# Attention and a clustering block on one core: stacking the first keys and queries inside SBUF, and moving five small steps of the attention

## The chip, the core and the metric

The kernel runs on one core of a Trainium2 chip, in one launch. The metric is the device time in microseconds (us); lower is better. The profile is one more execution, taken by the hardware profiler, with every instruction's start and end on each engine: PE is TensorE (matmuls; PEld its weight loads), DVE is VectorE, ACT is ScalarE, POOL is GpSimd, and SP is SyncE, which here only issues transfers. ACT and POOL can issue transfers too. "SPq", "ACTq" are the instructions with which an engine issues a transfer.

## The reference

Four images x of 256 channels and 64 x 64 points go through two layers. The first is self-attention over all 4096 points of an image, the second a clustering block with two group norms, an MLP and a pointwise convolution. All is float32.

```python
# layer 0, per image, xf = x as 256 x 4096
q = jnp.einsum('oc,bcn->bno', wq, xf) + bq              # 32 numbers a point
k = jnp.einsum('oc,bcn->bon', wk, xf) + bk[None, :, None]
attn = softmax(jnp.einsum('bnd,bdm->bnm', q, k), axis=-1)   # 4096 x 4096
v = jnp.einsum('oc,bcn->bon', wv, xf) + bv[None, :, None]
out = jnp.einsum('bcn,bmn->bcm', v, attn)
x = gamma[0] * out + x
# layer 1
y = x + ls1 * cluster(group_norm(x), ...)
y = y + ls2 * mlp(group_norm(y))
z = relu(batch_norm(y * dw_w)); z = relu(batch_norm(conv1x1(z, pw_w)))
```

The change touches only layer 0 (queries, keys, scores, softmax, and the product with the values).

## The kernel before, in words

The whole order of the work is written out by hand: each engine executes its instructions in the order of the program, and an engine waits (with everything behind it) until its next instruction may start. The compiler framework adds the waits, from which instruction writes or reads which tile.

**Queries and keys (L326 to L355).** For one image, the 4096 points are 8 blocks of 512 (`NB`). A projection (`projected`, L331) puts four blocks under each other, 32 rows each, into one 128 x 512 PSUM tile, so two projections of keys (i = 0, 1) and two of queries cover an image. `halves_of` splits each into a high part (float32r, ACT, L348) and a rest (DVE, L349), and writes four copies in a fixed pattern of high and low to DRAM (L355, four transfers of 256 KB). `k_unit` (L411) and `q_block` (L405) read one block back, whose 32 rows then lie interleaved by four on 128 partitions. One float32r matmul over these 128 rows gives the score with the cross terms of the two parts.

**Scores.** A unit u is one query block nb = u // 8 with one key block g = u % 8; there are 64 units an image (`units`). `half(u, h)` makes half of a unit's scores: two matmuls into one of the two `ps_s` PSUM buffers (`products`, L433), a copy to SBUF by ACT (`kept`, L446), and a running maximum over the keys by DVE (`highest_of`, L457), kept in the tile `top`. Starting unit u (`begun`) also issues the load of keys u + 1; the two `k` buffers alternate, so that load waits until PE is through with unit u - 1. A half that is "kept only" takes its maximum later, from the SBUF copy; such operations stand in the list `held`, and `caught(n)` issues the next n of them on DVE. `fold` (L514) catches all that are left and ends the maximum of a query block.

**The start (`alone`), image 0 only.** The value pairs (`v_pair`, L388: eight matmuls and an ACT copy L396; 16 pairs in all) 0 to 2, then `staged` (projection 0 of keys and queries, with its DRAM copies), the first loads of k and q, pairs 3 to 7, the sums of values that the product needs (`sums(g)`, four POOL operations L608 for each of 8 groups), then eight units of scores. In the first of them stand the second projections (`halved`, tag `t13`), and between them pairs 8 to 15, and the other weights (`load_rest`, a generator that issues a few SP transfers with every `next`; its last step has two POOL operations on the pointwise weights). Images 1 to 3 do this work inside the layer 1 of the image before.

**The weighting.** `weighting` runs 64 units. PE multiplies the values with the exponentials by a scheme of seven products for eight (`weigh`, parts 0 to 3, L678), from which results `av` are evicted by ACT at the end of a query block (`evict`, L708) and combined by POOL (`combined`, L719 to L724). In unit u, `exps(u + 1)` subtracts the maxima (DVE, L599 twice; the maxima lie in half of the PSUM tile `hold`, which takes one of the two `ps_s` buffers) and takes exponentials (ACT, L603 to L605), and `factors(u + 1)` forms the sums: t on DVE (L622), s and t4 on POOL (L608), and the running sum of the denominators `acc` (POOL). Between the parts the scores of later units are put in (`due`): two halves a unit, three in units 1, 3, 7 and 9, which are then kept only.

**Maxima and denominators of a block.** For query blocks from the third on, `highest(nb + 1)` (in unit g = 5 and 6) reduces `top` across partitions through small transposes in the tile `few`, writes 512 numbers to DRAM (L99) and reads them back on all partitions (`mr`, L100); ACT copies `mr` into `hold` (L582). `total(nb - 1)` does the same with the denominators, from g = `when` on. `few` takes the buffer of the weights `mix` (pool `swap`); the first call of `spare`, which is in `total(0)` in unit 10, lets POOL clear it (L539). `leave` multiplies by the denominators (POOL, L748), `sent` stores the result to DRAM (SP, L756).

**The tail.** In the last dozen units `load` (L106, SP) brings x in again, `shift` (ACT, L766) adds a constant, and `back` (POOL's queue, accumulating) adds the stored result.

Of the kernel before, what the change touches and what calls it, by code (L numbers as in the profile page):

```python
# [8 lines left out]
F32 = mybir.dt.float32  # L9
F32R = mybir.dt.float32r  # L10
# [4 lines left out]
P = 128  # L15
# [3 lines left out]
NB = 512  # L19
# [41 lines left out]
def attention_then_cluster_block(  # L61
# [101 lines left out]
    def load_rest():  # L163
        load_mix("first")
        yield
        nc.sync.dma_start(out=fvb[:, ED:], in_=v_b.partition_broadcast(P))
        nc.sync.dma_start(out=wproj_s[:ED], in_=wproj)
        nc.sync.dma_start(out=wproj_s[ED:, :], in_=pc[:, ipb : ipb + 1].rearrange("c o -> o c"))
        yield
        for i, f in enumerate(behind):  # L170
            f()
            if i == 2:
                yield
        nc.gpsimd.tensor_tensor(pw_q[1], pw_q[1], pw_q[3], ALU.add)
        nc.gpsimd.tensor_scalar(pw_q[3], pw_q[3], -1.0, None, ALU.mult)
        yield
# [88 lines left out]
    def wf():  # L265

        tps = ps_m.tile([P, NB], F32, tag="m", name="wf_p")
        for k in range(KC):
            nc.tensor.transpose(
                tps[:ED, k * P : (k + 1) * P], own_w["mix"][:, k, 0, 16 : 16 + ED], ident  # L270
            )
        nc.tensor.matmul(tps[:, C : C + ED], fb_w, ident[:ED, :ED], start=True, stop=True)
        nc.scalar.copy(wf_t, tps[:ED, :C])
        nc.scalar.copy(fvb[:, :ED], tps[:, C : C + ED])
# [43 lines left out]
    def attention(b, xs, ys):  # L318
# [7 lines left out]
        def projected(which, i, ps):  # L326

            col = 1 if which == "k" else 0
            for k in range(KC):
                for r in range(RG):  # L330
                    nc.tensor.matmul(  # L331
                        ps[r * D : (r + 1) * D],
                        wqk_s[:, k, col],
                        block(xs, k, 4 * i + r),
                        start=(k == 0),
                        stop=(k == KC - 1),
                    )

        def halves_of(which, i, hi, lo, ps, dma=nc.sync):

            col = 1 if which == "k" else 0
            if which not in own:
                own[which] = dram.tile([NBLK // RG, P, 4, NB], F32, tag=which, name=f"{which}_{b}")
            bias = bqk_s[:, col : col + 1]
            nc.scalar.activation(hi, ps, AF.Identity, bias=bias)  # L348
            nc.vector.scalar_tensor_tensor(  # L349
                lo, ps, bias, hi.bitcast(F32), ALU.add, ALU.subtract  # L350
            )
            rows = own[which][i]
            for c in range(4):
                part = hi if c in ((0, 2) if which == "k" else (0, 1)) else lo
                dma.dma_start(out=rows[:, c], in_=part.bitcast(F32))  # L355

        def stacked(which, nb):

            i, r = divmod(nb, RG)
            return own[which][i, r * D : (r + 1) * D].rearrange("d c n -> (d c) n")  # L360

        def staged(name, which, dma=nc.sync):


            st = spool.tile([P, 4, NB], F32R, tag="s", name=f"st_{b}_{name}")
            ps = ps_s.tile([P, 2, NB], F32, tag="s", name=f"pr_{b}_{name}")
            for j, (w, i) in enumerate(which):
                projected(w, i, ps[:, j])
            for j, (w, i) in enumerate(which):
                halves_of(w, i, st[:, 2 * j], st[:, 2 * j + 1], ps[:, j], dma)  # L370

        def halved(which, i):

            ps = ps_m.tile([P, NB], F32, tag="m", name=f"{which}p_{b}_{i}")
            two = work.tile([P, 2, NB], F32R, tag="t13", name=f"hl_{which}_{b}_{i}")
            projected(which, i, ps)
            halves_of(which, i, two[:, 0], two[:, 1], ps)

        vps = {}

# [17 lines left out]
        def v_pair(i):  # L398
            v_half(2 * i)
            v_half(2 * i + 1)  # L400

        def q_block(nb):

            qs[nb] = work.tile([P, NB], F32R, tag="q", name=f"q_{b}_{nb}")
            nc.sync.dma_start(out=qs[nb].bitcast(F32), in_=stacked("q", nb))  # L405

        def k_unit(u):

            g = u % GRP
            ks[u] = big.tile([P, NB], F32R, tag="k", bufs=2, name=f"k_{b}_{u}")  # L410
            nc.sync.dma_start(out=ks[u].bitcast(F32), in_=stacked("k", g))  # L411

        def begun(u):

            if u in slots:
                return
            nb, g = divmod(u, GRP)
            if u + 1 < units:
                k_unit(u + 1)

            pool, tag = {SLOTS: (swap, "w1"), SLOTS + 1: (swap, "w2")}.get(
                u % (SLOTS + 2), (spool, "s")
            )
            slots[u] = pool.tile([P, 4, 2, QW], F32, tag=tag, name=f"s_{b}_{u}")
            if g == 0:
                tops[nb] = work.tile([P, 2, NB], F32, tag="top", bufs=1, name=f"top_{b}_{nb}")
# [18 lines left out]
        def kept(u, h, sc):  # L445
            nc.scalar.copy(slots[u][:, PAIR[h]].rearrange("p h r n -> p r h n"), tiles(sc))  # L446
# [314 lines left out]
        def load(i):  # L761
            ys.append(load_x(b, i))
# [46 lines left out]
        def alone():  # L809

            roots()
            for i in range(3):
                v_pair(i)
            staged("first", (("k", 0), ("q", 0)))
            k_unit(0)
            q_block(0)
            q_block(1)
            for i in range(3, 8):
                v_pair(i)
            for g in range(4):  # L820
                for f in sums(g):
                    f()
            for u in range(GRP):
                if u == 0:
                    begun(0)
                    halved("k", 1)
                    halved("q", 1)
                    rest = load_rest()
                half(u, 0)()
                if u < GRP - 1:  # L830
                    half(u, 1)()
                else:

                    sc = products(u, 1)
                    highest_of(0, tiles(sc))
                    kept(u, 1, sc)
                    v_pair(14)
                if u < 6:
                    v_pair(u + GRP)
                elif u == 6:  # L840
                    wf()
                if u > 1:
                    next(rest, None)
            fold(0)
            for g in range(4, GRP - 1):
                for f in sums(g):
                    f()
            tp = turned_over(0, ps_m.tile([P, 4, P], F32, tag="m", name=f"tt_{b}_0"))
            half(GRP, 0)
            dgs["dg"] = across(0, "w2", tp)  # L850
            spread(0, dgs["dg"])
            v_pair(15)
            exps(0)
            factors(0)
            half(GRP, 1, True)
            for f in sums(GRP - 1):
                f()
# [32 lines left out]
        def weighting(next_x, fill, early, begin):  # L890
# [6 lines left out]
            def tail(u):  # L897


                for at_u, f in (  # L900
                    (units - 12, lambda: load(0)),
                    (units - 11, lambda: load(1)),
                    (units - 10, lambda: (load(2), back(0))),
                    (units - 9, lambda: (load(3), back(1))),
                    (units - 8, lambda: back(2)),
                    (units - 5, lambda: (next_x(), next_x())),
                    (units - 4, lambda: (load_mix(b), next_x())),
                    (units - 4, lambda: b == B - 1 and load_mlp(b)),
                    (units - 3, lambda: (next_x(), begin())),
                    (units - 2, lambda: b < B - 1 and load_mlp(b)),  # L910
                ):
                    if u == at_u:
                        f()

            for u in range(units):
# [12 lines left out]
                maxima = due(u, 0)  # L928
                if more and nb and g == GRP - 2:
                    next(peak)  # L930
                    sent(nb - 1)
                if g == GRP - 1 and more:
                    gather(nb)
# [4 lines left out]
                if nb < 2 or g == 6:  # L938
                    caught(1)

                when = 1 if nb > 1 else 2
                if nb and g == when:
                    den = total(nb - 1)
                    next(den)
# [4 lines left out]
                    next(peak)  # L949
                if early and nb > 1:  # L950
                    early.pop(0)()
                if u in views:
                    pooled(views[u])
                    seen(views[u], (0,))
# [36 lines left out]
                    f()  # L991
                if nb and g == when:
                    next(den)
                elif nb and g == (4 if more else 3):
                    leave(nb - 1)
                elif nb and g == 4 and not more:
                    sent(nb - 1)
                if (u, 0) in at and (u, 1) in at:
                    caught(1)
                weigh(u, av, 3)  # L1000
                if g == 3 and nb + 2 < NBLK:
                    q_block(nb + 2)
# [1058 lines left out]
```

## Time and profile before

| | us |
|---|---|
| median of three runs | 3167.59 (3166.77 to 3168.53) |
| profiled execution, its own time | 3166.07 |
| its span from first to last instruction | 3164.3 |
| PE busy in the span | 3058.6 |
| DVE, POOL, ACT busy | 2510.8, 2321.1, 1779.7 |
| start to the last maximum of the first query block | 66.5 |
| a unit of weighting, from block 2 on | 7.0 |
| 256 KB of keys from DRAM, issue to landing | 2.7 |

A row of the timeline gives the start, the duration (of a merged piece: from its first start to its last end), the engine, the line in the code, the operation, "written<-read", the shapes, the count, and in brackets how long the engine had stood idle and which engine's instruction ended the wait. In the groups and waits the releaser is the one that came last by the profile. The clock column is the share of the full TensorE clock that was granted.

### The profile page before, as it was taken

Reading aid. Unit: us, or ns where it says so; the run is one execution under the profiler, and the core shown is the slowest. Engines: PE = TensorE matmul, PEld = TensorE weight load, DVE = VectorE, ACT = ScalarE, POOL = GpSimd, SP = SyncE. Lnnn points to the kernel's source line nnn. Section 1 sums busy time; section 2 is a strip of 40 time slices with the busy share of each in tenths; the row PEclk is TensorE's granted clock in tenths of the full one; section 3 lists DMA queues with packets and bytes.
Section 4 is the critical chain, followed back from the end, with each engine's and each line's share of the span. In section 5 each row is a group of like instructions: output and inputs, shape, how many; then the busy total and the mean of one; then the engine's idle time right before and its main releaser. Section 6 shows DMA issues by size and latency. Waiting matters only on the chain.

```text
span 3164.3 us, 41331 instructions
## 1 busy us (share of the span) xinstructions
PE 3058.6 (97%) x14210; PEld 2499.2 (79%) x14210; DVE 2510.8 (79%) x3574; ACT 1779.7 (56%) x2817; POOL 2321.1 (73%) x2216
## 2 busy tenths in 40 slices
PE   7999999999999999999999999999999999998999
PEld 5788888788678888778867888887877788885786
DVE  3889888677788888877778888787778888887675
ACT  4566664544556666454555666644555666655444
POOL 3888888377488888647758888855866888893663
PEclk9999999999999999999999999999999999999999
DMA  5112126100111222610011211441011122150000
GB/s 166 44 58 64 54 64 191 60 28 28 44 44 57 67 61 87 168 57 18 28 50 48 66 56 58 120 129 57 28 40 44 54 61 64 57 150 3 14 21 27
DMA packets 105875, 200.41 MB, mean 63 GB/s; under 512 B 14416, under 2 KB 30400, under 8 KB 104128
## 3 DMA queue, kind: packets, MB, share of 16 engines
q1 hardware_dynamic: 101856, 181.94, 18.1%
q0 software_dynamic: 2976, 14.70, 2.4%
q8 instruction: 113, 1.85, 0.2%
q10 hardware_dynamic: 832, 1.11, 0.1%
q14 instruction: 98, 0.80, 0.1%
HBM read 149.37 MB, written 48.34 MB: 62 GB/s over the span
## 4 chain that ended last, share of the span: by engine, by line
PE 68%; POOL 14%; DVE 10%; issue 3%; DMA 2%; ACT 2%; SPq 0%; POOLq 0%; ACTq 0%; DVEq 0%
PE av L678 29%; PE mo L1673 10%; PE sc L433 6%; POOL acc L608 5%; PE hq L1756 5%; PE hp L1756 3%; POOL t L608 3%; PE hr L1756 3%; PE fv L1245 3%; POOL s L608 2%; DVE top L457 2%; PE vp L388 2%; DVE s L599 1%; PE mo L1657 1%; DVE t L622 1%
## 5 line engine op out<-in xcount | busy, mean ns | idle before, releaser
L446 ACT COPY s<-sc 128x1024 f32<-128x1024 f32 x512 | 515.0, 1011 | 419.5 <-PE sc L433 411.0
L599 DVE TENSOR_TENSOR s<-s,hold 128x1024 f32<-128x1024 f32 x512 | 598.7, 1209 | 12.4 <-ACT hold L582 10.3
L608 POOL TENSOR_TENSOR acc<-acc,t 128x512 f32<-128x512 f32 x408 | 536.2, 1334 | 0.0
L678 PE MATMUL av<-s,v 128*128 128x256 f32 x2048 | 526.1, 379 | 6.6 <-ACT t L708 4.0
L678 PE MATMUL av<-s,sum 128*128 128x256 f32 x2048 | 526.8, 380 | 3.6 <-POOL s L608 3.4
L678 PE MATMUL av<-t,v 128*128 128x256 f32 x2048 | 526.8, 380 | 1.8 <-POOL t L608 1.8
L608 POOL TENSOR_TENSOR s<-t,s 128x512 f32<-128x512 f32 x256 | 339.7, 1327 | 251.5 <-DVE t L622 184.7
L622 DVE TENSOR_TENSOR t<-s,hold 128x1024 f32<-128x1024 f32 x256 | 312.0, 1219 | 205.3 <-POOL acc L608 108.7
L678 PEld LDWEIGHTS av<-s,v 128*128 128x128 f32 x2048 | 386.9, 189 | 70.3 <-ACT t L708 5.6
L433 PE MATMUL sc<-q,k 128*128 128x512 f32 x1024 | 395.1, 470 | 47.6 <-DVE top L457 27.9
L457 DVE TENSOR_TENSOR top<-sc,top 128x1024 f32<-128x1024 f32 x350 | 426.6, 1219 | 14.4 <-ACT s L446 10.4
L678 PEld LDWEIGHTS av<-t,v 128*128 128x128 f32 x2048 | 387.7, 190 | 61.5 <-POOL t L608 6.5
L678 PEld LDWEIGHTS av<-s,sum 128*128 128x128 f32 x2048 | 388.1, 190 | 60.9 <-POOL s L608 8.4
L1711 ACT ACTIVATE hs<-hs,pv_s 128x256 f32<-128x256 f32 x496 | 232.5, 502 | 352.5 <-DVE hs L1747 352.5
L1673 PE MATMUL mo<-hs,w 128*128 128x256 f32 x1512 | 384.8, 381 | 0.0
L608 POOL TENSOR_TENSOR t<-s 128x512 f32<-128x512 f32 x256 | 340.6, 1331 | 47.1 <-PE av L678 34.1
L1673 PEld LDWEIGHTS mo<-hs,w 128*128 128x128 f32 x1512 | 283.7, 190 | 46.9 <-ACT hs L1711 6.3
L603 ACT ACTIVATE hold<-s 128x512 f32<-128x512 f32 x256 | 154.1, 602 | 245.7 <-DVE s L599 245.3
L433 PEld LDWEIGHTS sc<-q,k 128*128 128x128 f32 x1024 | 175.0, 191 | 143.2 <-DVE top L457 85.4
L605 ACT ACTIVATE s<-s 128x1024 f32<-128x1024 f32 x256 | 266.8, 1042 | 0.0
L1747 DVE TENSOR_TENSOR hs<-hq,hs 128x256 f32<-128x256 f32 x496 | 198.7, 421 | 85.7 <-PE hq L1756 75.4
L678 PE MATMUL av<-t,sum 128*128 128x256 f32 x1024 | 262.4, 378 | 0.0
(292 smaller groups left out, 4862.3 us busy)
## 6 DMA issues: line engine op xcount, KB each, us to landing
k<-k SPq DMA_DIRECT2D x256, 256.0 KB, 2.7
x<-in_x SPq DMA_DIRECT2D x62, 512.0 KB, 5.6
out<-xn SPq DMA_DIRECT2D x62, 256.0 KB, 2.1
att<-t SPq DMA_DIRECT2D x56, 256.0 KB, 4.1
x<-att POOLq DMA_DIRECT2D x12, 1024.0 KB, 9.0
q<-q SPq DMA_DIRECT2D x32, 256.0 KB, 4.1
w<-in_w SPq DMA_DIRECT2D x8, 1024.0 KB, 12.0
k<-hl_k SPq DMA_DIRECT2D x28, 256.0 KB, 2.6
```

The costliest lines, as they stand in the source:

```text
L433: nc.tensor.matmul(sc[:, r, :], k_s[:, (2 * h + r) * P : (2 * h + r + 1) * P], qs[u // GRP], start=True, stop=True,)
L446: nc.scalar.copy(slots[u][:, PAIR[h]].rearrange("p h r n -> p r h n"), tiles(sc))
L457: nc.vector.tensor_tensor(top, src, top if saved[nb] is None else saved[nb], ALU.max)
L599: nc.vector.tensor_tensor(sh, sh, mb.to_broadcast([P, 2, 2, QW]), ALU.subtract)
L605: nc.scalar.activation(s[:, PAIR[1]], s[:, PAIR[1]], AF.Exp)
L608: nc.gpsimd.tensor_tensor(out, x, y, op)
L622: nc.vector.tensor_tensor(t31[u], s[:, B11 : B22 + 1 : 2], b12.to_broadcast([P, 2, 2, QW]), ALU.add)
L678: nc.tensor.matmul(av[bank][:, half_ * QW : (half_ + 1) * QW], a[:, r], t[:, r], start=(g == 0 and r == 0 and i in (1, 7, 2, 4)), stop=(g ...
L1673: return nc.tensor.matmul(bank[:, half * HB : (half + 1) * HB], a[:, j], t, start=start, stop=stop)
L1711: nc.scalar.activation(src, src, AF.Gelu_apprx_tanh, bias=pvc("b1", P, j + 4 * (i > 1)))
L1747: nc.vector.tensor_tensor(dst, ps, term, ALU.add)
L1756: nc.tensor.matmul(out, w, x, start=True, stop=True)
```

## The change

Five things are done, in the functions printed above.

- **Start.** `staged` no longer writes the first keys and queries to DRAM and reads them back: four transfers from SBUF to SBUF of 32 rows each (`straight`) put k_0, four q_0 (two of these issued by ACT) and four k_1 in place. The copies in DRAM are written after that (`written`), for the other blocks. The second projections stand in units 0 and 1, value pairs 6 and 7 too; later pairs, group 3's sums, q_1's load and `load_rest` are placed anew.
- **`spare()`** is called in unit 4 of the weighting.
- **First denominators:** `when` is 3, not 2, for query block 1; their `leave` is in g = 5, not 4.
- **Held maxima:** the `caught(1)` at the end of the units with three halves (1, 3, 7, 9) is gone.
- **`load(1)`** is called in unit 54, after the read of `mr` has been issued and ahead of `sent`, not at the end of unit 53.

```diff
--- before.py
+++ after.py
@@ -336,7 +336,7 @@
                         stop=(k == KC - 1),
                     )
-        def halves_of(which, i, hi, lo, ps, dma=nc.sync):
+        def halves_of(which, hi, lo, ps):
@@ -349,32 +349,54 @@
             nc.vector.scalar_tensor_tensor(
                 lo, ps, bias, hi.bitcast(F32), ALU.add, ALU.subtract
             )
+        def part_of(which, c, hi, lo):
+            return (hi if c in ((0, 2) if which == "k" else (0, 1)) else lo).bitcast(F32)
+        def written(which, i, hi, lo):
             rows = own[which][i]
             for c in range(4):
-                part = hi if c in ((0, 2) if which == "k" else (0, 1)) else lo
-                dma.dma_start(out=rows[:, c], in_=part.bitcast(F32))
+                nc.sync.dma_start(out=rows[:, c], in_=part_of(which, c, hi, lo))
         def stacked(which, nb):
             i, r = divmod(nb, RG)
             return own[which][i, r * D : (r + 1) * D].rearrange("d c n -> (d c) n")
-        def staged(name, which, dma=nc.sync):
-            st = spool.tile([P, 4, NB], F32R, tag="s", name=f"st_{b}_{name}")
-            ps = ps_s.tile([P, 2, NB], F32, tag="s", name=f"pr_{b}_{name}")
-            for j, (w, i) in enumerate(which):
-                projected(w, i, ps[:, j])
-            for j, (w, i) in enumerate(which):
-                halves_of(w, i, st[:, 2 * j], st[:, 2 * j + 1], ps[:, j], dma)
+        def staged():
+            st = spool.tile([P, 4, NB], F32R, tag="s", name=f"st_{b}")
+            ps = ps_s.tile([P, 2, NB], F32, tag="s", name=f"pr_{b}")
+            both = {"k": (st[:, 0], st[:, 1]), "q": (st[:, 2], st[:, 3])}
+            for j, w in enumerate("kq"):
+                projected(w, 0, ps[:, j])
+            def straight(w, dst, r, other=nc.sync):
+                for c in range(4):
+                    (other if c % 2 else nc.sync).dma_start(
+                        out=dst[c::4].bitcast(F32), in_=part_of(w, c, *both[w])[r * D : (r + 1) * D]
+                    )
+            for g in range(2):
+                ks[g] = big.tile([P, NB], F32R, tag="k", bufs=2, name=f"k_{b}_{g}")
+            qs[0] = work.tile([P, NB], F32R, tag="q", name=f"q_{b}_0")
+            halves_of("k", *both["k"], ps[:, 0])
+            straight("k", ks[0], 0)
+            halves_of("q", *both["q"], ps[:, 1])
+            straight("q", qs[0], 0, nc.scalar)
+            straight("k", ks[1], 1)
+            for w in "kq":
+                written(w, 0, *both[w])
         def halved(which, i):
             ps = ps_m.tile([P, NB], F32, tag="m", name=f"{which}p_{b}_{i}")
             two = work.tile([P, 2, NB], F32R, tag="t13", name=f"hl_{which}_{b}_{i}")
             projected(which, i, ps)
-            halves_of(which, i, two[:, 0], two[:, 1], ps)
+            halves_of(which, two[:, 0], two[:, 1], ps)
+            written(which, i, two[:, 0], two[:, 1])
         vps = {}
@@ -415,7 +437,7 @@
             if u in slots:
                 return
             nb, g = divmod(u, GRP)
-            if u + 1 < units:
+            if u + 1 < units and u + 1 not in ks:
                 k_unit(u + 1)
             pool, tag = {SLOTS: (swap, "w1"), SLOTS + 1: (swap, "w2")}.get(
@@ -811,21 +833,14 @@
             roots()
             for i in range(3):
                 v_pair(i)
-            staged("first", (("k", 0), ("q", 0)))
-            k_unit(0)
-            q_block(0)
-            q_block(1)
-            for i in range(3, 8):
+            staged()
+            for i in range(3, 6):
                 v_pair(i)
-            for g in range(4):
+            for g in range(3):
                 for f in sums(g):
                     f()
+            rest = load_rest()
             for u in range(GRP):
-                if u == 0:
-                    begun(0)
-                    halved("k", 1)
-                    halved("q", 1)
-                    rest = load_rest()
                 half(u, 0)()
                 if u < GRP - 1:
                     half(u, 1)()
@@ -834,13 +849,23 @@
                     sc = products(u, 1)
                     highest_of(0, tiles(sc))
                     kept(u, 1, sc)
+                if u == 6:
+                    wf()
+                elif u == 7:
                     v_pair(14)
-                if u < 6:
-                    v_pair(u + GRP)
-                elif u == 6:
-                    wf()
-                if u > 1:
+                else:
+                    v_pair(u + 6)
+                if u < 2:
+                    k_unit(u + 2)
+                    halved("kq"[u], 1)
+                elif u == 2:
+                    q_block(1)
+                    for f in sums(3):
+                        f()
+                else:
                     next(rest, None)
+                    if 3 < u < 6:
+                        v_pair(u + 8)
             fold(0)
             for g in range(4, GRP - 1):
                 for f in sums(g):
@@ -899,7 +924,6 @@
                 for at_u, f in (
                     (units - 12, lambda: load(0)),
-                    (units - 11, lambda: load(1)),
                     (units - 10, lambda: (load(2), back(0))),
                     (units - 9, lambda: (load(3), back(1))),
                     (units - 8, lambda: back(2)),
@@ -928,6 +952,8 @@
                 maxima = due(u, 0)
                 if more and nb and g == GRP - 2:
                     next(peak)
+                    if u == units - 10:
+                        load(1)
                     sent(nb - 1)
                 if g == GRP - 1 and more:
                     gather(nb)
@@ -938,7 +964,8 @@
                 if nb < 2 or g == 6:
                     caught(1)
-                when = 1 if nb > 1 else 2
+                when = 1 if nb > 1 else 3
                 if nb and g == when:
                     den = total(nb - 1)
                     next(den)
@@ -949,6 +976,8 @@
                     next(peak)
                 if early and nb > 1:
                     early.pop(0)()
+                if u == 4:
+                    spare()
                 if u in views:
                     pooled(views[u])
                     seen(views[u], (0,))
@@ -991,12 +1020,10 @@
                     f()
                 if nb and g == when:
                     next(den)
-                elif nb and g == (4 if more else 3):
+                elif nb and g == (5 if nb == 1 else 4 if more else 3):
                     leave(nb - 1)
                 elif nb and g == 4 and not more:
                     sent(nb - 1)
-                if (u, 0) in at and (u, 1) in at:
-                    caught(1)
                 weigh(u, av, 3)
                 if g == 3 and nb + 2 < NBLK:
                     q_block(nb + 2)
```

## The prediction

> **What bounds the kernel now.** I read the page first: it says which engine is full.
>
> ```profile
> span 3164.3 us, 41331 instructions
> PE 3058.6 (97%) x14210; PEld 2499.2 (79%) x14210; DVE 2510.8 (79%) x3574; ACT 1779.7 (56%) x2817; POOL 2321.1 (73%) x2216
> PE 68%; POOL 14%; DVE 10%; issue 3%; DMA 2%; ACT 2%; SPq 0%; POOLq 0%; ACTq 0%; DVEq 0%
> ```
>
> TensorE (PE) is busy 97% of the span, so only time in which PE stands still can be won. The rest is 106 us, 9.5 of it the wait for the first load. So next I read the timeline of PE alone, for matmuls with an idle time in front. Around units 9 to 11 of each image's attention stand the same ones (in images 1 to 3 they start at 945 and 950, 1722 and 1727, 2475 and 2480); here is image 0, all engines:
>
> ```profile
> 157.28 1.84 DVE L457 TENSOR_TENSOR top<-s,top 128x1024 f32<-128x1024 f32 x1 [1.06 <-ACT s L446]
> 159.04 2.34 DVE L599 TENSOR_TENSOR s<-s,hold 128x1024 f32<-128x1024 f32 x2
> 161.30 1.21 DVE L457 TENSOR_TENSOR top<-sc,top 128x1024 f32<-128x1024 f32 x1
> 162.57 0.74 PE L433 MATMUL sc<-q,k 128*128 128x512 f32 x2 [1.09 <-DVE top L457]
> 164.15 0.42 POOL L539 MEMSET few<- 128x384 f32 x1
> 164.60 0.69 DVE L545 TENSOR_REDUCE few<-few 128x16 f32<-128x512 f32 x1 [1.47 <-POOL few L539]
> 167.60 0.73 PE L433 MATMUL sc<-q,k 128*128 128x512 f32 x2 [1.71 <-DVE top L457]
> ```
>
> To be seen: during the weighting only one score buffer turns over, so a score matmul waits for VectorE (DVE) to have read the last one. DVE, in order, first stood for a ScalarE (ACT) copy (1.06), then for GpSimd's (POOL's) clearing of `few` (1.47); PE paid 1.09 and 1.71. Third, units 54 to 56, again alike in all images:
>
> ```profile
> 475.01 0.84 SPq L106 DMA_DIRECT2D x<-in_x  x2
> 475.91 0.42 SPq L100 DMA_DIRECT2D mr<-row_mx  x1
> 481.53 0.59 ACT L582 COPY hold<-mr 128x512 f32<-128x512 f32 x1 [2.54 <-DMA mr<-row_mx]
> 487.32 1.13 PE L678 MATMUL av<-s,v 128*128 128x256 f32 x4 [0.84 <-ACT t L708]
> ```
>
> The broadcast of the maxima is issued behind 1 MB of x and takes 5.6 us to its reader (192.38 to 196.06, 3.7, where nothing is ahead of it). Last the start:
>
> ```profile
> 33.44 1.20 PE L433 MATMUL sc<-q,k 128*128 128x512 f32 x4
> 36.17 1.22 DVE L457 TENSOR_TENSOR top<-sc,s 128x1024 f32<-128x1024 f32 x1 [1.12 <-ACT s L446]
> 42.94 2.05 PE L433 MATMUL sc<-q,k 128*128 128x512 f32 x4 [3.03 <-DMA k<-k]
> 65.68 0.79 DVE L514 TENSOR_TENSOR top<-top 128x512 f32<-128x512 f32 x1
> ```
>
> The first maxima run from 36.2 to 65.7: fifteen at 1.22 are 18.3 us, so DVE is half idle, waiting for scores, and these for keys.
>
> [...] after 39.9 to 42.9 idle, the granted clock is 0.50 from 43 to 48. [...] The trace of before has no transfer from one SBUF tile to another.
>
> **The change, part by part.** The sum is made on the profiled execution: span 3164.3, 3166.1 in all, 1.5 under the median of 3167.6.
>
> *Start.* Projections end at 21.1 in both. Before: eight writes of 256 KB to DRAM issued 21.9 to 26.5, k_0 read back at 26.8, q_0 at 30.7, first score 33.44. After: SP issues four k_0 pieces (0.53 each, 2.10 for four of the same form), then two of q_0; ACT issues the other two. q's low half is written at 24.15, so the last q_0 piece goes at about 24.7. A piece of 64 KB is not in the trace: 1.3 (the 2 KB row's landing) to 2.7 (256 KB)[...]. I take 2.7: first score at 27.4, 6.0 earlier. The two ACT issues (0.6 each) hold up three value copies behind them; the sixth value pair waits 1 us, hidden by that landing. From there PE must do what it did earlier: per unit two scores (0.45 each when back to back) and a value pair (1.73), and 1.85 for each second projection, put in units 0 and 1, two pairs in units 4 and 5. Following this by hand, with each score buffer free 0.45+1.01+1.22 after its start, the fold comes 31.3 after the first score, at 58.7; before it was 32.2 (with 3.0 idle and some 2.6 lost to half clock). That is 6.9. But the DMA engines: from 27.3 on, 4 MB of writes and 1 MB of k_2, k_3, k_4, q_1 must pass before unit 4 starts at 42.8; at 330 GB/s (217 to 382 in the windows from 34 to 42) that is 15.3, plus 2 to land: 44 to 45. So I take 2.0 off: **4.9**, from 3 to 7. POOL's sums for groups 4 to 6 end some 9.4 after the last weights (issued at about 49.4, landed by 53), well before the first factor needs POOL (76.4 - 6). The moved value pairs, group-3 sums and small loads lie beside this and cost nothing else; without that cover they would be 0.8 a piece on POOL.
>
> *Held maxima.* The end-of-unit call in units 1, 3, 7, 9 is gone: one maximum each (1.22 to 1.84, and about 1 of waiting for the ACT copy issued just before). The held operations move to the next units, where the instruction order of the changed kernel puts them between the subtraction and the t addition: there DVE waits for exponentials anyway (1.15 in most units). Gone by this: 2.2 of the 2.42 before the score at 98.08, and 0.48 at 114.20, in image 0; 0.68 and 1.09 in units 8 to 10; in images 1 to 3 0.25+0.47+0.68+1.07, 0.26+0.48+0.69+1.08, 0.48+0.68+1.10.
>
> *Clearing and denominators.* The clearing (0.42 on POOL) goes to unit 4, where POOL stood 2.25 for DVE (116.59). The 1.47 is gone, and with the denominators one unit later the 1.71, 1.71, 1.71, 1.73. The multiplication by them (2.36 on POOL) moves from unit 12 to 13, at its end, after unit 14's factors: done by about 191.7 on before's clock less 3.5. Behind it on SP waits the store of t, and behind that k_27; k_27 lands at 195.4 and is needed at 199; the store must land before the next evictions at 198.5, and does at 196. Slack 2.5, so nothing is charged.
>
> Held maxima and denominators together: 6.2 + 4.2 + 4.2 + 4.0 = 18.6. Is there room? Units 7 to 12 take 48.7, of which PE idles 4.3, so PE needs 44.4. DVE needs 6 x (2.35 + 1.22) + 14 x 1.22 for maxima, 2.4 more for six that read SBUF beside POOL (1.7 against 1.22), 2.1 for the reductions: 43.0. It fits, barely, so I count 85%: **15.8**.
>
> *Load behind the broadcast.* mr now lands about 2 us earlier; its reader then waits no more than the exponentials in front of it. PE gets back 0.84, 0.84, 1.51, 0.83; 90% of 4.0 is **3.6**. x_1 is issued 1.3 later, 12 us ahead of its use at 488.67, and the store behind it on SP is read two units later.
>
> Sum 4.9 + 15.8 + 3.6 = 24.3: 3167.6 - 24.3 = **3143.3**.
>
> **Rivals.** *A, the start buys nothing:* keys 2 to 4 come when they came, PE idles for them and falls to half clock. For: DMA share 1.0 from 34 to 42. Against: the first score needs neither. 3148.2.
> *B, DVE is the bound of units 7 to 12:* its 43.0 leaves no room for waits on ACT and POOL, and PE's idle only moves. For: DVE 11.49 of 13.20 busy, POOL 12.96, from 149.4 to 162.6. Against: the moved maxima fill waits. It loses 85% of 13.9: 3155.1.
> *C, the stacking transfers are serial:* should a 32-partition transfer run on one DMA engine (382/16 = 24 GB/s, 2.7 us each), twelve take 33; keys 2 come at about 64 instead of 42.9, +20, just what the rest wins (19.4). At 5.6 each, the landing of the 32-row bias loads, twelve take 67 and the total is about 3202. It decides from 2.7 each. [...]
> *D, the waits come back* as PE waiting for POOL (12.96 of 13.20 busy in units 9 and 10), and A holds too: within 6 of before, 3164.
>
> **Numbers.** Forecast 0.63, A 0.17, B 0.13, D 0.03, C 0.04. The measurement can tell 0.2%, 6.3 us, from no change. Faster: the first three, 0.93; same 0.03; slower 0.04. Range: all of the start (2.0 more), the full 18.6 and 4.0, and 4 unseen give 3136; B with some of the start lost gives 3156. **3136 to 3156.**
>
> **What would show it.** First score near 27.4 and fold near 60; clock 1.0 from 40 to 50; no PE idle over 0.5 in units 8 to 11 of any image; `few` cleared in unit 4; ACT's copy of mr 3.7 after its issue. I am wrong if the first score comes after 33, if idle before scores in those units stays over 1, or if PE waits for POOL's s or t there.

## The result, and the profile after

Beside each other on one chip, five runs each: before 3167.49 us (3166.17 to 3168.53), after **3137.74 us** (3135.16 to 3139.37). The ratio is 0.9906, 95% interval [0.9891, 0.9920]: 29.75 us less. The profiled execution of the changed kernel took 3139.37 (span 3137.6) and is the slowest of its five, so between the two traces only 26.7 us can be followed.

The page of the changed kernel, the three lines that answer to those of before:

```profile
span 3137.6 us, 41318 instructions
PE 3052.5 (97%) x14210; PEld 2498.7 (80%) x14210; DVE 2513.1 (80%) x3574; ACT 1779.3 (57%) x2817; POOL 2318.8 (74%) x2216
PE 74%; DVE 8%; POOL 8%; ACT 3%; issue 3%; DMA 2%; SPq 0%; ACTq 0%; POOLq 0%; DVEq 0%
```

The engines do what they did. What changed is the chain that ended last: POOL's part of it fell from 14% to 8%, PE's rose from 68% to 74%.

The timeline of image 0 around units 4 and 9 to 11, in the changed kernel:

```profile
111.05 0.41 POOL L561 MEMSET few<- 128x384 f32 x1
...
157.07 0.81 PE L455 MATMUL sc<-q,k 128*128 128x512 f32 x2
160.24 0.73 PE L455 MATMUL sc<-q,k 128*128 128x512 f32 x2
163.50 0.70 DVE L566 STREAM_TRANSPOSE few<-rden 128x512 f32<-128x512 f32 x1
164.24 0.69 DVE L567 TENSOR_REDUCE few<-few 128x16 f32<-128x512 f32 x1
164.07 0.81 PE L455 MATMUL sc<-q,k 128*128 128x512 f32 x2
167.26 0.72 PE L455 MATMUL sc<-q,k 128*128 128x512 f32 x2
```

`few` is cleared in unit 4, the reduction follows its transpose without a wait, and no score matmul has a bracket: the waits of 1.09 and 1.71 are gone, in all four images. Here is the broadcast of the maxima in unit 54:

```profile
467.92 0.33 SPq L100 DMA_DIRECT2D mr<-row_mx  x1
468.36 0.84 SPq L106 DMA_DIRECT2D x<-in_x  x2
472.33 0.59 ACT L604 COPY hold<-mr 128x512 f32<-128x512 f32 x1 [1.34 <-DVE t L644]
```

x_1 now stands behind the broadcast. Its reader comes 4.4 after the issue, not 5.6, and what it waits for last is DVE, no longer the transfer. Last the start:

```profile
27.02 1.16 PE L455 MATMUL sc<-q,k 128*128 128x512 f32 x4
...
37.77 1.17 PE L455 MATMUL sc<-q,k 128*128 128x512 f32 x4 [1.30 <-DMA k<-k]
41.32 1.57 PE L455 MATMUL sc<-q,k 128*128 128x512 f32 x4 [0.65 <-DMA k<-k]
46.68 1.17 PE L455 MATMUL sc<-q,k 128*128 128x512 f32 x4 [2.06 <-DMA k<-k]
...
62.94 1.01 DVE L536 TENSOR_TENSOR top<-top 128x512 f32<-128x512 f32 x1
66.73 2.04 PE L611 MATMUL hold<-dg,ones 128*128 128x512 f32 x2 [1.54 <-DVE dg L550]
68.57 3.62 PE L410 MATMUL vp<-wv_s,x 128*128 128x256 f32 x8
...
73.91 2.08 PE L700 MATMUL av<-s,v 128*128 128x256 f32 x8 [1.26 <-ACT s L626]
```

The first score comes at 27.02, 6.4 earlier. The fold at 62.94 is only 2.74 earlier: PE waits 4.0 for keys 2, 3 and 4. And the first weighting matmul, 73.91, is 0.24 earlier than before's 74.15, for the pieces at 66.73 and 68.57 take twice the time (2.04 and 3.62) that they took in before (1.10 and 1.89). The windows of that stretch tell both reasons (columns: busy time of PE, PEld, DVE, ACT, POOL, then granted clock, DMA share, GB/s):

```profile
34.00:38.00 4.00, 2.70 (x20) 0.87 (x19) 2.70 (x3) 1.67 (x3) 2.19 (x3) 1.00 0.98 330
38.00:42.00 4.00, 3.35 (x14) 2.22 (x13) 2.35 (x3) 2.51 (x3) 0.00 (x0) 1.00 1.04 376
...
64.00:68.00 4.00, 2.37 (x8) 1.48 (x9) 1.79 (x2) 1.45 (x2) 3.73 (x5) 0.66 0.00 0
68.00:72.00 4.00, 4.00 (x10) 2.72 (x10) 2.35 (x2) 0.00 (x0) 0.00 (x0) 0.50 0.00 0
```

From 34 to 42 the DMA engines are full (share 0.98 and 1.04, 330 and 376 GB/s); from 64 to 72 the clock falls to 0.66 and 0.50.

**Where the 26.7 came from**, read from the times of the same exponential of the same unit in both traces: the start 0.26; units 0 to 12 of the four images 7.10, 5.90, 5.91 and 5.94, together 24.85; from unit 55 to the first group-norm matmul 0.27, 0.20, 1.06 and 0.39, together 1.9; all the rest -0.3.

### The profile page after: what moved, and what is told of

Read it like the earlier page. It is cut to its first block, busy times and chain, and to the rows that moved or that the text cites. A ratio compares the mean times of both kernels' runs of the same rounds, so it can differ in the third digit from the quotient of the medians.

```text
span 3137.6 us, 41318 instructions
## 1 busy us (share of the span) xinstructions
PE 3052.5 (97%) x14210; PEld 2498.7 (80%) x14210; DVE 2513.1 (80%) x3574; ACT 1779.3 (57%) x2817; POOL 2318.8 (74%) x2216
## 3 DMA queue, kind: packets, MB, share of 16 engines
q1 hardware_dynamic: 101904, 181.81, 18.6%
## 4 chain that ended last, share of the span: by engine, by line
PE 74%; DVE 8%; POOL 8%; ACT 3%; issue 3%; DMA 2%; SPq 0%; ACTq 0%; POOLq 0%; DVEq 0%
PE av L700 35%; PE mo L1700 10%; PE sc L455 7%; PE hq L1783 5%; PE hp L1783 3%; PE hr L1783 3%; PE fv L1272 3%; POOL acc L630 3%; PE vp L410 2%; POOL t L630 2%; DVE s L621 1%; POOL s L630 1%; PE mo L1684 1%; DVE top L479 1%; DMA w<-in_w 1%
## 5 line engine op out<-in xcount | busy, mean ns | idle before, releaser
L479 DVE TENSOR_TENSOR top<-sc,top 128x1024 f32<-128x1024 f32 x350 | 427.0, 1220 | 26.7 <-ACT s L468 22.9
L630 POOL TENSOR_TENSOR t<-s 128x512 f32<-128x512 f32 x256 | 331.1, 1293 | 45.6 <-PE av L700 32.2
## 6 DMA issues: line engine op xcount, KB each, us to landing
w<-in_w SPq DMA_DIRECT2D x8, 1024.0 KB, 10.6
```

The lines of the kernel that those rows point to most:

```text
L479: nc.vector.tensor_tensor(top, src, top if saved[nb] is None else saved[nb], ALU.max)
L630: nc.gpsimd.tensor_tensor(out, x, y, op)
```

## The experiments

The theory: the start buys almost nothing, for keys 2 to 4 wait for bytes and the half clock falls on the chain behind the fold; the weighting gives nearly all, more than the idle times show. The rival: the start gives its 4.9 and the rest the rest. A second question was whether the edits of the weighting work one by one.

**The start alone, and all but the start.**

```diff
# start_only: before, with only the new staged, straight, written, alone
# no_start: after, with staged, halves_of and alone of before
-            staged()
+            staged("first", (("k", 0), ("q", 0)))
...
```

> The kernel before with the new start alone. Theory (keys 2 to 4 wait for the DMA engines, and a stretch at half clock falls on the chain from the fold to the first weights): the first weighting matmul comes within 1 us of where it was, 74.15, and the time is 3165 to 3168. Rival 1 (the start is worth what the prediction gave it): 4.9 less, 3162.6, first weighting matmul near 69.3. Rival 2 [...]: a spread of several us between the runs, with a mean gain of 1 to 3.

> The changed kernel with the start of before. Theory: the weighting gives it nearly all, 26 to 29 less than before: 3138 to 3141, no more than 3 above the changed kernel. Rival (start 4.9, the rest 24.8): 3142.6. If parts help one another, it and the start alone do not add up to the 29.75 of the whole.

Measured: the start alone 0.9995 [0.9987, 1.0003], 1.6 us less (from 1.0 more to 4.1 less); all but the start 0.9913 [0.9898, 0.9928], the same as the whole change. In the trace of the start alone the first weights came 1.7 earlier, more than the theory's 1, and by unit 5 this was 0.6 later than before (clock 0.71 from 72 to 76, 0.79 from 96 to 104). So the start as it stands is worth little: 4.9 is outside the interval, no gain at all is inside it. The second rival's small gain with a wide spread (9 us over 13 runs) fits best.

**The held maxima alone, and the clearing with the denominators alone.**

```diff
# held_only, on before
-                if (u, 0) in at and (u, 1) in at:
-                    caught(1)
# sparewhen_only, on before
-                when = 1 if nb > 1 else 2
+                when = 1 if nb > 1 else 3
+                if u == 4:
+                    spare()
-                elif nb and g == (4 if more else 3):
+                elif nb and g == (5 if nb == 1 else 4 if more else 3):
```

> The kernel before without the end-of-unit call for the held maxima in units 1, 3, 7 and 9. By the prediction's sum of idle times: 4.45 + 2.47 + 2.51 + 2.26 = 11.7 less, 3155.8. Theory (each wait ahead of a score costs about 0.29 more than the idle time shown, and four or five go in each image): 5 more, about 16 in all, 3151. Rival (DVE has no room and the waits move to the clearing and the denominators of units 9 to 11): under 8.

> The kernel before with the clearing in unit 4 and the first denominators one unit later, alone. By the idle times of the prediction: 1.71 four times, 6.9 less, 3160.6. Theory (each wait costs 0.29 more): 8, 3159.5. Rival (the held maximum at the end of unit 9 still stands ahead of everything, so that DVE is late anyway): 3 or less, 3164.5.

Measured: 0.9986 [0.9978, 0.9994] and 0.9985 [0.9979, 0.9992], 4.4 and 4.8 less. In units 0 to 13 the traces give 4.9 and 4.2; the whole change gives 24.9 there. The 4.2 holds a loss of 2.2 in the first units of image 0, where the clock was low (0.89 and 0.69 from 92 to 100); from unit 11 to 12, where the edit acts, 1.6 is gained in each image, 6.4 in all, near the 6.9 of the idle times. So **neither gives the most of it by itself**: 9 to 11 apart, 25 together. My expectation for the held maxima (11.7 or 16) was wrong and its rival right. The trace of the held maxima alone, image 1, shows how it is lost:

```profile
944.69 0.42 POOL L539 MEMSET few<- 128x384 f32 x1
945.15 0.69 DVE L545 TENSOR_REDUCE few<-few 128x16 f32<-128x512 f32 x1 [2.40 <-POOL few L539]
...
948.15 1.22 PE L433 MATMUL sc<-q,k 128*128 128x512 f32 x2 [3.21 <-DVE top L457]
```

and the windows of that kernel, the same columns as above:

```profile
930.00:945.15 15.15, 14.71 (x66) 12.13 (x65) 11.49 (x11) 9.04 (x11) 14.75 (x12) 1.00 0.19 53
...
948.00:952.00 4.00, 3.85 (x11) 3.19 (x12) 3.81 (x6) 2.51 (x4) 3.92 (x4) 0.62 0.00 0
```

Up to unit 11 this kernel is as far ahead as the whole change (4.96 gained since unit 0 in image 1). Then DVE reaches the transpose ahead of the clearing 3.3 sooner, counted from unit 0, but POOL its clearing only 2.4 sooner: it is full (14.75 of 15.15), and the clearing stands at the end of its queue. The wait grows from 1.47 to 2.40 on DVE and from 1.71 to 3.21 on PE, and the clock falls to 0.62 behind it. Of the 4.96, 0.99 is left by unit 13. This trace is of the slowest of the 13 runs (3168.95, median 3162.08), and has the lowest clock (0.988). The four runs with a clock of 0.995 or more took 3152.7 to 3157.3, 9 to 13 less than before's median: much of what this kernel loses goes with the clock, and how much differs from run to run.

**Clearing or denominators?** Two kernels undo one of them in the changed kernel.

```diff
# spare_back
-                if u == 4:
-                    spare()
# when_back
-                when = 1 if nb > 1 else 3
+                when = 1 if nb > 1 else 2
-                elif nb and g == (5 if nb == 1 else 4 if more else 3):
+                elif nb and g == (4 if more else 3):
```

> The changed kernel with the clearing of few back where few is first used, which is now unit 11. Theory (with the held maxima gone from the ends of units, TensorE reaches the reductions earlier, but GpSimd does not, and the clearing stands at the end of GpSimd's queue, so VectorE and with it TensorE wait for it): the wait of some 2 to 3 before a score returns in units 10 to 12 of every image, and 3 to 4 of each image's 5.9 are lost: 3150 to 3154. Rival (it was the denominators' place, not the clearing): no wait for GpSimd, time within 2 of the changed kernel's 3138.

> The changed kernel with the first denominators back in unit 10 and their multiplication in unit 12. Theory (the clearing is what matters): without it the two reductions of 0.7 stand ahead of a maximum, one wait of up to 1 before a score returns in unit 10 or 11, so 0 to 1.3 an image: 3138 to 3143. Rival (the place matters as much as the clearing): 1.71 and more an image, 3145 to 3152.

Measured: 0.9964 [0.9951, 0.9976] with the clearing back, 11.4 less than before where the whole change has 29.75; 0.9915 [0.9902, 0.9929] with the denominators back. In units 0 to 13 of the traces: 2.6 and 20.7 of the 24.9. So the clearing of 0.42 us decides 22, the place of the denominators 4 (1.1 an image), each while all the others are in. The wait for POOL is there again with the clearing back, image 1:

```profile
946.48 0.41 POOL L561 MEMSET few<- 128x384 f32 x1
946.92 0.69 DVE L567 TENSOR_REDUCE few<-few 128x16 f32<-128x512 f32 x1 [3.45 <-POOL few L561]
...
949.93 1.22 PE L455 MATMUL sc<-q,k 128*128 128x512 f32 x2 [3.17 <-DVE top L479]
```

I had said 3 to 4 an image for it; it is 5 to 6, since the wait comes to 3.45 on DVE, and the granted clock falls behind it here too (0.53 from 1724 to 1728 in image 2).

**The load alone undone.**

```diff
# load_back: after, with
-                    if u == units - 10:
-                        load(1)
+                    (units - 11, lambda: load(1)),
```

> The changed kernel with x_1's load back at the end of unit 53. Theory from the trace (the waits for ACT's t at the end of block 6 return: the exponentials of units 55 to 63 shift by 0.94, 0.18, 2.04 and 0.38, of which the last eviction keeps about 2.0 in all): 2 above the changed kernel, about 3139.7. Rival (the prediction's 3.6): 3141.3. Second rival (nothing, the end of the block waits for something else): equal to it.

Measured: 0.9910 [0.9897, 0.9924]; 2 us can't be told from none by the time. The traces tell it: with the load back, PE's waits for ACT's t return (0.83 at 477.62, 1.55 at 2022.66), and from unit 55 to the group norm nothing is gained (-0.02, -0.10, -0.07, -0.05), where the changed kernel gains 1.9. The size is the theory's 2, not 3.6. At unit 56 the changed kernel is 1.20 ahead in image 0; by the end of the block PE waits for POOL's s and t in more places (0.18 and 0.22 at 483.84, 502.55), and 0.27 is left.

**Why the start buys nothing: bytes, or clock?** Three kernels on the changed one: the queries' DRAM copies later; idle PE filled with matmuls that nobody reads; both.

```diff
# q_later
-            for w in "kq":
-                written(w, 0, *both[w])
+            written("k", 0, *both["k"])        # written("q", 0), then q_block(1), in unit 3
...                                             # written("q", 1) in unit 4
# busy: n of these at each place that the expectation lists
+                nc.tensor.matmul(t[:, :C], wv_s[:, 0, :P], xs[0][:, 0, :C], start=True, stop=True)
# q_later_busy: the first, and the second from unit 7 on
```

> The changed kernel with the DRAM copies of the queries (2 MB) written behind the load of the fifth keys instead of ahead of the third. Theory (keys 2 to 4 wait because 4 MB of copies share the DMA engines with them): the waits of 1.30, 0.65 and 2.06 ahead of the scores of units 2 to 4 shrink to under 1 together, the fold comes 3 to 4 earlier than 62.94, near 59.5, and the time is 2 to 4 lower, about 3134.5. Rival 1 (each key load pays its own two steps through DRAM, whatever else moves): fold within 1 of 62.94, time the same. Rival 2 (the fold comes earlier, but the half clock behind it eats the gain): fold near 59.5, first weighting matmul within 1 of 73.91, time the same within 1.

> The changed kernel with matmuls of 128x256 that nothing reads put where TensorE waits in the start: 5, 2 and 8 ahead of the scores of units 2, 3 and 4, 8 in unit 7, 7 ahead of the transposes of the maxima, 6 ahead of the broadcast of them, 4 ahead of the first weights. It leaves nothing out. Theory (the half clock comes from TensorE's low share of work between 56 and 66): granted clock 1.0 from 56 to 80, the value pair behind the broadcast 1.9 instead of 3.62, first weighting matmul near 72 instead of 73.91, time 1 to 3 lower, runs closer together. Rival [...]: still half at 60 to 76, time the same or up to 1 higher.

> The two together, with the added matmuls from unit 7 on. If both theories hold: first weighting matmul near 68, time 4 to 6 below the changed kernel, 3132 to 3134, the start then worth what the prediction gave it. If the start's gain is lost elsewhere anyway (later waits in units 0 to 5 for keys, queries or POOL's sums): first weighting matmul near 68 and less than 2 of it left at unit 12.

Measured: 0.9916 [0.9902, 0.9930], 0.9917 [0.9904, 0.9931] and 0.9922 [0.9910, 0.9935]: no gain. With the queries' copies later, keys 2 to 4 wait 1.5 instead of 4.0, but now keys 5 wait:

```profile
46.39 0.32 SPq L430 DMA_DIRECT2D q<-q  x1
47.80 0.41 SPq L436 DMA_DIRECT2D k<-k  x1
...
52.65 1.16 PE L458 MATMUL sc<-q,k 128*128 128x512 f32 x4 [2.98 <-DMA k<-k]
```

That is my edit's own fault: the read of q_1 waits on SP for the queries' copies, and the load of keys 5 (42.93 in the changed kernel) stands behind it. The fold came at 64.98, so this run doesn't settle the theory. With PE filled the clock does stay up: at 1.00 in the whole start, with both edits from 56 on, while in each of the twelve traces without added matmuls it falls somewhere between 24 and 104 (to 0.50 from 44 to 48 in before, from 68 to 72 in the changed kernel). The value pair behind the broadcast takes 1.89 again instead of 3.62. But the added matmuls keep PE busy for 18.7 us, and the first weights came at 78.41, 4.5 later, and at 79.01 with both edits: the cure cost more than it saved.

**Fewer bytes ahead of the keys.** So the last start takes the bytes away.

```diff
# more_straight, on after; more_straight_only, the same start with the weighting of before
-            for w in "kq":
-                written(w, 0, *both[w])
...
                 if u < 2:
-                    k_unit(u + 2)
+                    own["stack"]("k", u + 2)   # four pieces of 64 KB from SBUF, as k_0
                     halved("kq"[u], 1)
+                    if u:
+                        own["later"][2]()      # copies of the second keys
...
+                    if u == 3:
+                        own["stack"]("q", 1)
+                    elif u == 5:
+                        own["later"][0]()      # copies of the first keys
+                    elif u > 5:
+                        own["later"][(1, 3)[u - 6]]()   # of the queries
```

> The changed kernel with keys 2 and 3 and query block 1 also stacked from SBUF, and of the copies in DRAM only the second keys' ahead of keys 4; the other three follow after keys 6. Theory (keys 2 to 4 wait for the bytes ahead of them, 4 MB then, 1 MB and eight pieces of 64 KB now): no wait of over 0.5 for keys 2 to 4, fold near 59.5 instead of 62.94, first weighting matmul at 67.5 to 71 instead of 73.91, of which what is left at unit 12 of image 0 is what the start is worth: 3 to 5 if the prediction's figure was only starved of bytes. Rival 1 (the wait only moves to later keys, as with the queries' copies alone): fold within 1 of 62.94. Rival 2 (a half clock takes it back): fold near 59.5, but less than 1.5 left at unit 12. In the time, 0 to 5 lower; runs differ by that much.

> The kernel before with the start of the last run alone (keys 2 and 3 and query block 1 stacked from SBUF too, three of the four copies in DRAM later), the weighting as before. Theory (the start is worth 5 to 6 by itself once no key waits for bytes): first weighting matmul near 68.3 instead of 74.15, and 4 to 6 lower, 3161.5 to 3163.5; with the start as in the change it was 1.6 (from 1.0 above to 4.1 below). Rival (the gain is taken back by waits or half clock in units 0 to 8, as the start alone gave back 1.72 by unit 5): first weighting matmul near 68.3, time under 2 lower.

Measured: **3131.74 us** (3131.24 to 3132.39), ratio 0.9888 [0.9873, 0.9903], the fastest of all; its interval overlaps the changed kernel's, but its runs (3131.2 to 3132.4) lie below all of that one's (3135.2 to 3139.4; on another chip, with before at 3167.49 there and 3167.59 here). With the weighting of before it is 0.9990 [0.9981, 0.9998], 3.2 less. The timelines from the fold to the first weights, of the faster kernel:

```profile
60.10 0.69 DVE L547 TENSOR_TENSOR top<-top 128x512 f32<-128x512 f32 x1
63.48 1.10 PE L622 MATMUL hold<-dg,ones 128*128 128x512 f32 x2 [1.07 <-ACT s L479]
64.41 1.89 PE L421 MATMUL vp<-wv_s,x 128*128 128x256 f32 x8
...
68.26 2.08 PE L711 MATMUL av<-s,v 128*128 128x256 f32 x8 [1.50 <-ACT s L637]
```

and with the weighting of before:

```profile
60.85 0.69 DVE L547 TENSOR_TENSOR top<-top 128x512 f32<-128x512 f32 x1
64.42 2.04 PE L622 MATMUL hold<-dg,ones 128*128 128x512 f32 x2 [0.91 <-DVE dg L561]
66.26 3.62 PE L421 MATMUL vp<-wv_s,x 128*128 128x256 f32 x8
...
71.60 2.08 PE L711 MATMUL av<-s,v 128*128 128x256 f32 x8 [1.24 <-ACT s L637]
```

Two things are shown. The bytes: keys 2 to 4 wait for no transfer any more, keys 5 for 0.74, and the fold comes at 60.10 and 60.85, about where the prediction had it. The clock: these two starts are the same instructions, and from the fold to the first weights one takes 8.2 and the other 10.8, because the half clock (0.50 from 64 to 68) hit only the second. It is worth 2.6 us. The faster kernel had its own (0.64 from 56 to 60) ahead of the fold, where PE waits for DVE's maxima anyway. Its first weights are 5.9 ahead of before's, and once image 0 has done unit 12 it is 4.5 further ahead than the changed kernel (11.9 against 7.4). Not all of this is the start: in this execution the projections ended 1.0 earlier than in before (20.07 and 21.11), and up to there the two programs are the same.

**What the clock does to the start, in all traces.** Three forms of the start ran without added matmuls in eleven kernels (the form of `q_later` ran in one more). Here are the times from the end of the first projections to the fold, and from there to the first weights, in us, each with the granted clock of the stretch:

| start | trace | projections to fold | clock | fold to first weights | clock |
|---|---|---|---|---|---|
| of before | before | 44.6 | 0.89 | 8.5 | 0.98 |
| | sparewhen_only | 42.4 | 1.00 | 8.4 | 1.00 |
| | held_only | 42.7 | 0.96 | 11.0 | 0.69 |
| | no_start | 42.2 | 1.00 | 10.6 | 0.68 |
| of the change | the changed kernel | 42.2 | 1.00 | 11.0 | 0.69 |
| | when_back | 41.5 | 1.00 | 10.7 | 0.68 |
| | start_only | 42.1 | 0.96 | 8.8 | 1.00 |
| | load_back | 43.2 | 0.93 | 8.8 | 0.97 |
| | spare_back | 43.5 | 0.93 | 8.8 | 0.97 |
| fewer bytes | more_straight | 40.0 | 0.96 | 8.2 | 0.97 |
| | more_straight_only | 39.7 | 1.00 | 10.8 | 0.68 |

At full clock up to the fold, the start of before takes 42.2 to 42.4, that of the change 41.5 to 42.2, that with fewer bytes 39.7. So the start as changed is worth 0 to 0.9 there, and with fewer bytes 2.5 to 2.7. The half clock on the chain behind the fold comes with each of the three starts, in two of four, two of five and one of two traces: that the change moved it there is not shown. The first weights come on average at 73.6 with the start of before and at 73.0 with that of the change.

## Why the prediction was right, and where not

It said 24.3 less, and 29.75 came, inside the range. It was right in sum with terms off in opposite directions, so in part by luck.

- **Start, 4.9: failed.** It measured 0.26 in the trace and 1.6 (-1.0 to 4.1) in time. Landing and first score were right (27.02 against 27.4; a piece of 64 KB landed in 2.1, where I had taken 2.7 from a span of 1.3 to 2.7). Two steps failed. The 2.0 taken off for the DMA engines was too little: keys 4 landed at 46.55, not at 44 to 45, as their read, issued at 41.19 among the queries' copies, took 5.36; and keys 2 and 3, which the sum left out, waited as well (the read of keys 2 was issued at 34.04, when the copies that it reads had landed), 4.0 in all. And the 2.6 that I counted as lost to half clock ahead of the fold was no property of the old start: two other traces of it have a clock of 1.00 there and take 42.2 and 42.4 from the projections to the fold, as the changed kernel does. "Clock 1.0 from 40 to 50" held; the half clock then fell on 65 to 72, on the chain from the fold to the first weights, and cost 2.5 us of this trace. By the table above that goes with the execution; it is not shown to be a price of the change. Keys that come hardly earlier are rival A's mechanism, for this term alone; A's time was missed because of the next one.
- **Held maxima, clearing and denominators, 15.8: too small.** 24.85 was measured in units 0 to 12. The mechanism was right: no PE idle over 0.5 is left in units 8 to 11, nor waits for POOL, and the free time on DVE was enough. Mis-sized were the 85% (nothing was lost, so 18.6), the waits under 0.3 that I had not counted (brackets removed in all: 20.3), and the price of a wait, 4.5 more over 26 waits fewer. This is what a bracket leaves out, in the changed kernel's PE timeline, a score that does not wait and one that does:

```profile
865.53 1.03 PE L700 MATMUL av<-s,sum 128*128 128x256 f32 x4
866.21 0.81 PE L455 MATMUL sc<-q,k 128*128 128x512 f32 x2
866.86 1.03 PE L700 MATMUL av<-t,v 128*128 128x256 f32 x4
868.12 0.73 PE L455 MATMUL sc<-q,k 128*128 128x512 f32 x2 [0.24 <-ACT s L468]
868.69 0.59 PE L700 MATMUL av<-s,v 128*128 128x256 f32 x2
```

  From weights to weights across a score: 1.33 without a wait (865.53 to 866.86), 1.83 with one (866.86 to 868.69). The wait costs 0.50, and its bracket says 0.24: without it the score starts 0.35 before the modelled end of the matmul ahead. On average over the 26 it was 0.17 beyond the bracket.
- **Load, 3.6: right place, half the size.** In the exponentials 3.9 were there at unit 56 and 3.5 at unit 63, 1.9 at the group norm. What became late next is, as far as the trace of image 0 shows, POOL's s and t in the last units. Its reader came 4.4 after the issue, not 3.7: DVE's t was then the last to come.
- **Rivals.** B and D (a wait for POOL in those units) did not happen with the whole change, but they are what happens with half of it: the held maxima without the clearing wait 3.21 on PE. I had costed them together without seeing that the gain of the held maxima is lost again where the clearing stays. C is out: the twelve pieces, issued from 21.48 on, had all landed by 30.76, 9.3 us, where one after the other they would have taken 33. Before's trace had shown nothing against C; these pieces are the first that do.

**Still open.** What sets where the half clock falls. Equal starts ran with and without it (from the fold to the first weights at 0.97 and 0.68 in the two with fewer bytes). A single long gap doesn't tell it: in the changed kernel the longest one from 24 to the half clock is 2.06, with PE busy 4.21 of the 8 us from 56 to 64. And the prediction's own example does not repeat: before's wait of 3.03 for keys 2 was followed by a clock of 0.50, but in two other traces of the same start waits of 2.88 and 2.66 at the same place were followed by 1.00. The half clock also comes and goes in layer 1 (0.50 at 608 in the changed kernel, 1.00 there in the one with PE filled), and the times of one kernel spread by 1 to 16 us over the runs; how much of the 3 us between the traces' 26.7 and the medians' 29.75 it makes was not tried.

## What to carry to other kernels

When work left the end of DVE's units in held_only, DVE came 3.3 us sooner to the transpose, and POOL, full with 14.75 of 15.15 us, only 2.4 sooner to its clearing: look for the full engine's small instruction that others wait for (here a clearing of 0.42), and put that where the engine has time. Edits that free the same stretch must be judged together, for each may be worth little while the other wait stands (here 4.9 and 4.2 us alone, 24.9 together). When a load is made earlier, count the bytes that stand ahead of the loads after it, not only its own landing (keys 4 took 5.36 us among the queries' copies, 2.7 is the median of all key loads). Before a stretch at half clock is booked as something to win, see whether it is there in other executions of the same code (the start of before has 0.89, 1.00, 0.96 and 1.00 ahead of the fold).

## Not expected of the hardware

- A score wait cost more than the idle time that the profile writes beside it: 0.50 for a bracket of 0.24 at 868.12 in the changed kernel, 24.85 for 20.3 in all.
- The granted clock fell to 0.50 (68 to 72 in the changed kernel) with no single PE gap over 2.1 us from 24 on, and one wait of 3.2 us (held_only, image 1) was followed by 0.62 in the next 4 us. The same start ran with and without the half clock behind the fold, 2.6 us apart.
- The clock lost (time times the share not granted) between 24 and 112 us was near a multiple of 1.71 us in each of the 14 traces: none with PE filled all through, once to three times that in the others (1.72 in more_straight, 3.40 in the changed kernel, 5.08 in before).
- Twelve 32-row pieces of 64 KB between SBUF tiles did not get in each other's way: 1.95 to 2.22 us each, issued 0.2 to 0.8 apart; only the last took 3.51, from a cause that stays open.

```profile
k<-st SPq DMA_DIRECT2D x8, 64.0 KB, 2.1
q<-st ACTq DMA_DIRECT2D x2, 64.0 KB, 2.1
```
